# Norms ahead of the weight split in the first block of queries, and the stores of key differences issued by ScalarE

## Chip, cores and metric

The kernel runs on one core of a Trainium2 chip. The metric is the device time of one execution in microseconds (us); lower is better. Before the change three executions took 1596.75, 1595.55 and 1596.62 us, so the median is 1596.62 us.

The core has five engines with a queue of instructions each, which run beside each other and wait for one another by semaphores: TensorE (PE in the profile; PEld is its weight load), VectorE (DVE), ScalarE (ACT), GpSimd (POOL) and SyncE (SP). An engine works through its own queue in order. In this kernel SP does nothing but issue DMA transfers, which move data between the core's memory (SBUF) and the chip's main memory (DRAM).

## What is computed

One transformer layer with adaptive layer norm on 2 x 1024 tokens of width 512: modulated norm, causal attention with 32 query heads and 8 key heads of width 64 and rotary positions, an output projection, a second modulated norm and a feed-forward part with ternary weights.

```python
mod = (_silu(c) @ wmod).reshape(2, 6, 1, -1)          # sa, ca, ga, sb, cb, gb
h = _layernorm(x) * (1 + ca) + sa
q = (h @ Wq) ...; k = (h @ Wk) ...; v = (h @ Wv) ...   # heads of 64
q = apply_rope(q, pos); k = apply_rope(k, pos)
scores = where(causal, q k^T / 8, min)
x = x + ga * (softmax(scores) v) @ Wo
h = _layernorm(x) * (1 + cb) + sb
x = x + gb * rms_norm(silu(h Wg) * (h Wu)) @ Wp        # Wg, Wu, Wp rounded to three levels by groups of 64
```

All of it is in float32. Each float32 operand of a large matrix product is split into a high part (the value rounded to the type float32r, by a copy on ScalarE) and a low part (the value minus its high part, by a subtraction on VectorE or GpSimd); three products of the parts, high x high, high x low and low x high, are summed in PSUM.

## The kernel before

The first stage, some 300 us of the span, makes queries, keys and values and stores them to DRAM for the attention stage, which reads them back in pieces. It works on four blocks of 512 tokens. For each block `keys_values(blk)` makes two tiles of keys (each four heads) and four tiles of values, and then, for blocks 0 to 2, `queries(blk, g)` makes the queries of one group of heads, for g = 0 to 7. The queries of block 3 and everything after are emitted by a planner with costs and due times, which does not see the first stage. The order on each engine in the first stage is the order of the calls in the program.

The steps that matter, by function:

- `load_x(blk)` loads the tokens of a block into the tile xt, one call ahead. `stats(blk, t)` (st, mv) and `rstd(blk)` measure mean and variance on VectorE; ve is the variance plus epsilon, and rs, its power -1/2, is one GpSimd instruction. `norm(blk, t)` normalises 128 tokens in place: one VectorE tensor_scalar on xt with mv and rs. Stats and rstd of the next block run at the end of `keys_values`; the norms of the next block run in the first two groups of queries, two in each (lines 535 to 537).
- `first_T(blk, e)` transposes the normalised xt on TensorE into the PSUM tile pt, in the groups 2 to 5; `first_h` modulates it on VectorE (h), copies the high part on ScalarE (hH) and takes the low part on GpSimd (hL).
- `split_w("wq", n)` splits a 512 KB piece of Wq, which arrives in the buffer stage: high part wqH on ScalarE, low part wqL on VectorE. It runs in block 0 alone, pieces 0 to 3 behind the four value tiles and pieces 4 to 7 in the groups 0 to 3 of queries. Each split frees a buffer, and SP then issues the next load.
- `rope_mm` makes two PSUM tiles pqk of a group or key tile in 24 matrix products; `rope_mul` multiplies them by cosines and sines (four VectorE products ra, rc, rb, rd) and joins them on GpSimd (ra and rc). For keys GpSimd also takes two differences of neighbouring 128-key steps, for the tile of differences kds.
- `rope_end(n)` finishes the group that is one behind: for each of ra and rc a ScalarE copy (rr, high part) and a VectorE subtraction (rr, low part), then four stores by SP (qs or ks). For keys there are more: a second ScalarE copy makes the high part of the differences in place (ra<-rb, rc<-rd), and SP stores it at line 479: two stores for each key tile, four for each block, sixteen in all (eight of 256 KB and eight of 192 KB).
- `value(blk, t)` makes a tile of values in the PSUM tile pv with 12 matrix products; ScalarE copies it to vt (three buffers), and SP stores it (vs).

PSUM tiles come from two rotating sets, four banks for the first half of pqk and small products, three banks for the second half, pt and pv. A bank must be read before TensorE can fill it again: so a copy vt or a product rb, rd that comes late holds TensorE up three tiles later.

The lines that the change touches, before:

```python
479                SY.dma_start(f32(half[:, to:to + 512 - f]), f32(r[:, f:512].bitcast(F32R)))
...
535        if blk < 3 and g < 2:
536            norm(blk + 1, 2 * g)
537            norm(blk + 1, 2 * g + 1)
538        rope_end(1)
```

Of the kernel before, what the change touches and what calls it, by code (L numbers as in the profile page):

```python
# [9 lines left out]
F32R = mybir.dt.float32r  # L10
# [181 lines left out]
def block_kernel(ctx, tc, x, wq, wk, wv, wo, wgu, wpj, cin, wmod, cos, sin, out):  # L192
    nc = tc.nc
    T = InOrder(tc, nc.tensor, True)
    V, A, P, SY = (InOrder(tc, e, False) for e in (nc.vector, nc.scalar, nc.gpsimd, nc.sync))
# [3 lines left out]
    def f32(ap):  # L199
        return ap.bitcast(F32)  # L200
# [51 lines left out]
    def put_q(dst, rr, h, tok):  # L252
        to = f32(dst[h // 2 * 64:h // 2 * 64 + 64, :, h % 2, tok:tok + 512]).rearrange("(c d) l t -> d l c t", c=2)
        SY.dma_start(to, f32(rr[h * 32:h * 32 + 32]).rearrange("d (l c) t -> d l c t", l=2))
# [99 lines left out]
    def mods(i, n):  # L354
        if n == 0:
            mod_row[i] = stile("pm")
        pm = mod_row[i]
        wm = staged.pop(0)
        for k in range(EC):
            T.matmul(pm[k * 32:k * 32 + 32, n * 256:n * 256 + 256], sc[:, k, :], wm[:, k, :], start=True, stop=True)  # L360
        if n == 0:
            stage()
        else:
            mod_row[i] = wm[:, 0:2, :].rearrange("p n e -> p (n e)")
            A.activation(mod_row[i], pm, AF.Copy)

    def mods_T(i):
        pm = stile("pmT")[:, 0:EC * B].rearrange("p (e b) -> p e b", b=B)
        for e in range(EC):
            T.matmul(pm[:, e, :], mod_row[i][:, e * 128:e * 128 + 128], pick, start=True, stop=True)  # L370
        stage()
        if i % 2:
            V.tensor_scalar(modT[:, i], pm, 1.0, None, ALU.add)
        else:
            V.tensor_copy(modT[:, i], pm)
# [9 lines left out]
    def split_w(name, n, width=256):  # L385
        nn = slice(n * width, n * width + width)
        if name == "wq":
            st = staged.pop(0)
        else:
            st = first[name][:, :, nn]  # L390
        split(st, wH[name][:, :, nn], wL[name][:, :, nn])
        if name == "wq":
            stage()
# [17 lines left out]
    def norm(blk, t):  # L411
        d = st_x[blk]
        V.tensor_scalar(d["x"][:, t, :], d["x"][:, t, :], d["mv"][:, t, 0:1], d["rs"][:, t:t + 1], ALU.subtract, ALU.mult)

    def first_T(blk, e):
        d = st_x[blk]
        if e == 0:
            d["h"] = [(hp0, hp1)[blk % 2].tile([128, EC, 512], F32R, name=n) for n in ("hH", "hL")]
        d["pt"] = d.get("pt", {})
        d["pt"][e] = transpose_x(d["x"], 4, e)  # L420

    def first_h(blk, e):
        d = st_x[blk]
        modulate(blk // 2, d["pt"].pop(e), lp, 0, *d["h"], e)
# [3 lines left out]
    def rope_mm(blk, name, c0, dst):  # L428
        hH, hL = st_x[blk]["h"]
        pt = [stile("pqk"), xtile([128, 512], "pqk")] if ropes or blk else [stile("pqk") for half in range(2)]  # L430
        parts = [(w_, h_, k) for w_, h_ in ((wH[name], hH), (wL[name], hH), (wH[name], hL)) for k in range(EC)]
        if not (ropes or blk):
            turns = [(half, part) for k in range(EC) for part in (parts[k], parts[EC + k]) for half in range(2)]
            turns += [(half, part) for part in parts[2 * EC:] for half in range(2)]
        else:
            turns = [(half, part) for half in range(2) for part in parts]
        seen = [0, 0]
        for half, (w_, h_, k) in turns:
            c = c0 + half * 128
            T.matmul(pt[half], w_[:, k, c:c + 128], h_[:, k, :], start=(seen[half] == 0), stop=(seen[half] == 3 * EC - 1))  # L440
            seen[half] += 1
        ropes.append([pt, blk % 2 * 512, dst])

    def rope_mul():
        pt, tok, dst = ropes[-1]
        c_, s_ = cs[:, tok:tok + 512], sn[:, tok:tok + 512]
        a, bb, c, d = (tp.tile([128, 512], F32, name=n) for n in ("ra", "rb", "rc", "rd"))
        V.tensor_tensor(a, pt[0], c_, ALU.mult)
        V.tensor_tensor(c, pt[0], s_, ALU.mult)
        V.tensor_tensor(bb, pt[1], s_, ALU.mult)  # L450
        V.tensor_tensor(d, pt[1], c_, ALU.mult)
        P.tensor_tensor(a, a, bb, ALU.subtract)
        P.tensor_tensor(c, c, d, ALU.add)
        ropes[-1][0] = (a, c)
        if len(dst.shape) == 3:

            ropes[-1][0] = (a, c, bb[:, 0:384], d[:, 0:384])
            for new, r in ((bb, a), (d, c)):
                P.tensor_tensor(new[:, 0:384], r[:, 128:512], r[:, 0:384], ALU.subtract)

    def rope_end(n):
        while len(ropes) > n:
            (a, c, *steps), tok, dst = ropes.pop(0)
            rr = tp.tile([128, 4, 512], F32R, name="rr")
            for i, r in enumerate((a, c)):
                A.activation(rr[:, i, :], r, AF.Copy)
                if not steps:
                    V.tensor_tensor(rr[:, 2 + i, :], r, f32(rr[:, i, :]), ALU.subtract)
                    continue
                V.tensor_tensor(rr[:, 2 + i, 0:128], r[:, 0:128], f32(rr[:, i, 0:128]), ALU.subtract)  # L470
                f, to = (128, 512) if tok else (0, 0)
                if not tok:

                    V.tensor_tensor(r[:, 0:128].bitcast(F32R), r[:, 256:384], f32(rr[:, i, 256:384]), ALU.subtract)
                high = r[:, 128:512].bitcast(F32R)
                A.activation(high, steps[i], AF.Copy)
                V.tensor_tensor(rr[:, 2 + i, 128:512], steps[i], f32(high), ALU.subtract)
                half = [x for pair in kds for x in pair][[x for pair in ks for x in pair].index(dst)][i]
                SY.dma_start(f32(half[:, to:to + 512 - f]), f32(r[:, f:512].bitcast(F32R)))
            for h in (0, 2, 1, 3):  # L480
                if len(dst.shape) == 4:
                    put_q(dst, rr, h, tok)
                else:
                    SY.dma_start(f32(dst[:, h, tok:tok + 512]).rearrange("(c d) t -> d c t", c=4), f32(rr[h * 32:h * 32 + 32]))
# [14 lines left out]
    def keys_values(blk):  # L499
        b = blk // 2  # L500
        if blk < 3:
            load_x(blk + 1)
        for i in range(2):
            rope_mm(blk, "wk", i * 256, ks[b][i])
            if blk == 0:
                split_w("wv", i)
            rope_mul()
            rope_end(1)
        for t in range(4):
            value(blk, t)  # L510
            if blk == 0:
                split_w("wq", t)
            if t == 0:
                rope_end(0)
            if blk < 3:
                stats(blk + 1, t)
        if blk < 3:
            rstd(blk + 1)

    def queries(blk, g):  # L520
        rope_mm(blk, "wq", g * 256, qs[blk // 2][g])
        nxt = blk < 3 and 2 <= g < 6
        if nxt:
            first_T(blk + 1, g - 2)
        if blk == 0 and g < 4:
            split_w("wq", g + 4)
        rope_mul()
        if blk == 1 and g < 2:
            for n in range(2):
                mods(2 + g, n)  # L530
        elif blk == 1 and g in (3, 4):
            mods_T(g - 1)
        if nxt:
            first_h(blk + 1, g - 2)
        if blk < 3 and g < 2:
            norm(blk + 1, 2 * g)
            norm(blk + 1, 2 * g + 1)
        rope_end(1)
# [47 lines left out]
    for blk in range(NT // 512):  # L586
        keys_values(blk)
        if blk < NT // 512 - 1:
            for g in range(KVH):
                queries(blk, g)  # L590
# [13 lines left out]
    tail, outer, norm, rest = ExitStack(), ExitStack(), ExitStack(), ExitStack()  # L604
# [1021 lines left out]
```

## Time and profile before

| | us |
|---|---|
| median of three executions | 1596.62 |
| profiled execution | 1598.2 |
| its span (first to last instruction) | 1596.3 |
| TensorE busy | 1548.1 |
| VectorE busy | 1175.4 |
| GpSimd busy | 863.0 |
| ScalarE busy | 697.8 |

In the timelines below a line has the start in us, the duration in us, the engine (SPq is SP's DMA issues), the line in the program (a helper records every operation, so it is always L39), the operation, what is written from what, its shape, and how many instructions were merged. In square brackets stands the idle time of the engine before it and who ended it. The duration of an issue on SPq is the time that SP's queue was taken by it, not that of the transfer. Durations of neighbours on one engine can overlap a little, as an instruction begins before the last has written its end; the distance of starts is then the better measure.

The table of waits gives, for an engine and what it computed, which instruction ended its idle time: us in total, times, longest. The view by windows gives, for stretches of time, the busy time of each engine, the clock granted to TensorE (1.00 is full speed) and the mean busy share of the 16 DMA engines.

### The profile page before, as it was taken

What the parts mean: (1) busy time and instruction counts of PE and PEld (TensorE: products, weight loads), DVE (VectorE), ACT (ScalarE), POOL (GpSimd) and SP (SyncE); (2) the same over time, 40 slices, a digit from 0 to 9 for tenths busy, and PEclk for the clock granted to TensorE, in tenths of its full rate; (3) what the DMA queues carried; (4) which work ended last, traced back from release to release, by engine and by line L of the source; (5) the groups of instructions that cost most, each with busy time, mean ns of one, the idle gap of its engine ahead of it and who ended that gap; (6) DMA issues with size and microseconds to landing.
All of it is one profiled execution on the core that took longest, in us unless ns stands there. A gap on an engine that the chain in (4) does not pass through costs nothing.

```text
span 1596.3 us, 26757 instructions
## 1 busy us (share of the span) xinstructions
PE 1548.1 (97%) x9028; PEld 1068.0 (67%) x9028; DVE 1175.4 (74%) x2468; ACT 697.8 (44%) x1349; POOL 863.0 (54%) x758
## 2 busy tenths in 40 slices
PE   8899998989999999999999999999999999999998
PEld 7777887745555555555555555477788887888886
DVE  6888887778777788888878888857888674443444
ACT  3322222146555556555555656634655432222221
POOL 4364556537666765765676675713323544444343
PEclk9999999999999999999999999999999999999999
DMA  7775758775555546655646555576777833020000
GB/s 247 243 201 173 225 150 230 227 182 163 154 146 150 143 125 172 167 157 141 169 123 172 146 150 144 161 244 198 251 216 246 288 102 136 1 79 1 11 16 27
DMA packets 206592, 250.55 MB, mean 157 GB/s; under 512 B 34932, under 2 KB 144500, under 8 KB 206456
## 3 DMA queue, kind: packets, MB, share of 16 engines
q1 hardware_dynamic: 206456, 248.85, 53.0%
q8 instruction: 71, 1.16, 0.3%
q14 instruction: 65, 0.53, 0.1%
HBM read 156.24 MB, written 92.02 MB: 156 GB/s over the span
## 4 chain that ended last, share of the span: by engine, by line
PE 70%; DVE 13%; DMA 6%; issue 5%; SPq 3%; ACT 2%; POOL 1%; DVEq 0%; ACTq 0%; POOLq 0%
PE pgu L39 15%; PE po L39 13%; PE pj L39 10%; PE pfo L39 7%; PE pqk L39 6%; PE pm L39 5%; DVE junk L39 3%; SPq L39 3%; PE pr L39 2%; DVE rr L39 2%; DMA k<-ks 1%; DMA t<-qs 1%; DVE mm L39 1%; DVE ra L39 1%; DVE rd L39 1%
## 5 line engine op out<-in xcount | busy, mean ns | idle before, releaser
L39 POOL TENSOR_TENSOR acc<-acc,e 128x512 f32<-128x512 f32 x202 | 266.0, 1328 | 61.6 <-DVE acc L39 47.7
L39 PE MATMUL po<-e,vt 128*64 128x512 f32 (+1 forms) x1280 | 268.0, 557 | 4.2 <-DVE mx L39 1.6
L39 PE MATMUL pgu<-h,gu 128*128 128x512 f32 x1024 | 244.3, 391 | 0.0
L39 PEld LDWEIGHTS pgu<-h,gu 128*128 128x128 f32 x1024 | 192.0, 188 | 39.8
L39 DVE CUSTOM_DVE_ANT_0 junk<-pm,cmask,mm 128x384 bf16<-128x384 f32 (+1 forms) x256 | 174.6, 682 | 57.7 <-PE pm L39 33.2
L39 PEld LDWEIGHTS po<-e,vt 128*64 128x64 f32 x1280 | 84.0, 136 | 154.8 <-issue 123.3
L39 PE MATMUL pm<-k,t 64*128 64x384 f32 (+3 forms) x768 | 167.1, 384 | 16.1 <-DVE mx L39 6.0
L39 POOL TENSOR_SCALAR_AFFINE_SELECT e<-e 128x512 f32<-128x512 f32 x128 | 88.3, 692 | 143.6 <-ACT e L39 140.9
L39 PEld LDWEIGHTS pm<-k,t 64*128 64x128 f32 x768 | 93.5, 185 | 105.6 <-issue 31.6
L39 POOL TENSOR_TENSOR s<-hm 128x512 f32<-128x512 f32 x59 | 68.7, 1164 | 163.3 <-DVE hm L39 163.1
L39 DVE CUSTOM_DVE_ANT_0 junk<-pm,cmask 128x128 bf16<-128x128 f32 (+3 forms) x256 | 124.6, 487 | 41.4 <-PE pm L39 18.8
L39 DVE TENSOR_REDUCE mm<-pm 128x1 f32<-128x384 f32 (+2 forms) x256 | 128.3, 546 | 31.6 <-PE pm L39 31.1
L39 PE MATMUL pj<-woH,oh 128*128 128x512 f32 x512 | 142.2, 399 | 0.0
L39 POOL TENSOR_TENSOR on<-on,ri 128x512 f32<-128x512 f32 x64 | 85.5, 1337 | 66.8 <-DMA ri<-linv 62.7
L39 DVE TENSOR_TENSOR mL<-hm,mH 128x512 fp32r<-128x512 f32 x64 | 75.9, 1186 | 60.7 <-ACT mH L39 60.7
L39 DVE TENSOR_TENSOR hm<-gs,pgu 128x512 f32<-128x512 f32 x64 | 43.9, 686 | 94.3 <-PE pgu L39 89.9
L39 PEld LDWEIGHTS pj<-woH,oh 128*128 128x128 f32 x512 | 95.1, 188 | 20.9 <-issue 2.3
L39 ACT ACTIVATE mH<-hm 128x512 fp32r<-128x512 f32 x64 | 40.4, 632 | 146.1 <-PE pfo L39 133.3
L39 POOL TENSOR_TENSOR ra<-ra,rb 128x512 f32<-128x512 f32 x40 | 51.7, 1291 | 94.4 <-DVE rb L39 82.5
L39 PE MATMUL pfo<-pj,mH 128*128 128x512 f32 x256 | 100.4, 392 | 0.0
L39 PE MATMUL pfo<-pj,mL 128*128 128x512 f32 x256 | 99.7, 389 | 0.0
L39 POOL TENSOR_TENSOR sq<-sq,s 128x512 f32<-128x512 f32 x59 | 80.8, 1369 | 4.5
(1485 smaller groups left out, 3667.6 us busy)
## 6 DMA issues: line engine op xcount, KB each, us to landing
qs<-rr SPq DMA_DIRECT2D x128, 256.0 KB
t<-qs SPq DMA_DIRECT2D x64, 512.0 KB
k<-ks SPq DMA_DIRECT2D x64, 256.0 KB
ri<-linv SPq DMA_DIRECT2D x128, 128.0 KB
os<-on SPq DMA_DIRECT2D x64, 256.0 KB
ks<-rr SPq DMA_DIRECT2D x32, 256.0 KB
w<-in_wgu SPq DMA_DIRECT2D x32, 256.0 KB
gus<-wr SPq DMA_DIRECT2D x32, 256.0 KB
```

Source lines behind the costliest of these rows:

```text
L39: ins = f(*a, **k)
```

## The change

Two edits. In `rope_end` the sixteen stores of the key differences are issued from ScalarE's queue instead of SP's. In `queries`, for block 0 alone, the two norms of the next block's tokens in the groups 0 and 1 stand right behind the call of `rope_mm`, ahead of the split of Wq and of `rope_mul`; in blocks 1 and 2 they stay where they were. No instruction is added or removed, and what is computed is the same.

```diff
@@ rope_end
-                SY.dma_start(f32(half[:, to:to + 512 - f]), f32(r[:, f:512].bitcast(F32R)))
+                A.dma_start(f32(half[:, to:to + 512 - f]), f32(r[:, f:512].bitcast(F32R)))
@@ queries
         nxt = blk < 3 and 2 <= g < 6
+        if blk == 0 and g < 2:
+            norm(blk + 1, 2 * g)
+            norm(blk + 1, 2 * g + 1)
         if nxt:
             first_T(blk + 1, g - 2)
...
-        if blk < 3 and g < 2:
+        if 0 < blk < 3 and g < 2:
             norm(blk + 1, 2 * g)
             norm(blk + 1, 2 * g + 1)
         rope_end(1)
```

On VectorE the order from the end of block 0's values on was: ve, split piece 4, products of group 0, norms 0 and 1, split piece 5, products of group 1, norms 2 and 3, the two subtractions rr of group 0, split piece 6. It becomes: ve, norms 0 and 1, split piece 4, products of group 0, norms 2 and 3, split piece 5, products of group 1, the two subtractions, split piece 6. On ScalarE each store stands directly behind the copy that fills its tile (ra<-rb or rc<-rd), and ahead of rr<-rc or of the copy vt. On SP the sixteen issues are gone, and the others keep their order. TensorE's and GpSimd's orders stay as they were, and so does everything that the planner emits.

## The prediction

> **What bounds the kernel now.** I read the page's shares first: TensorE is busy 97% of the span, so only places where it stands still, and what makes it late there, can move the time. The change touches the projection of keys and queries, which ends near 300 us. So the second view is the table of what TensorE waited for in the first 300 us (total, times, longest, in us).
>
> ```profile
> PE 1548.1 (97%) x9028; PEld 1068.0 (67%) x9028; DVE 1175.4 (74%) x2468; ACT 697.8 (44%) x1349; POOL 863.0 (54%) x758
> ...
> PE pt L39 <- DVE xt L39: 6.0, 3, 4.3
> PE pm L39 <- DMA t<-qs: 5.3, 1, 5.3
> PE pv L39 <- DVE rd L39: 2.0, 1, 2.0
> PE pv L39 <- ACT vt L39: 1.0, 1, 1.0
> ```
>
> Four stops: transposes wait for the last norms at 58.9 to 64.6; the third value tile of block 1 waits for VectorE at 113.90; the last value tile of block 2 waits for ScalarE's copy of the first at 191.08; the attention's first scores wait for loads at 275 to 281. The third view, the order of time on VectorE, says which of them counts.
>
> ```profile
> 52.33 0.17 DVE L39 TENSOR_SCALAR ve<-mv 128x4 f32<-128x4 f32 x1
> 52.41 1.23 DVE L39 TENSOR_TENSOR wqL<-stage,wqH 128x1024 fp32r<-128x1024 f32 x1
> ...
> 55.95 2.63 DVE L39 TENSOR_SCALAR xt<-xt,mv,rs 128x512 f32<-128x512 f32 x2
> ...
> 62.03 2.56 DVE L39 TENSOR_SCALAR xt<-xt,mv,rs 128x512 f32<-128x512 f32 x2
> 64.52 0.68 DVE L39 TENSOR_TENSOR rr<-ra,rr 128x512 fp32r<-128x512 f32 x1
> 65.12 0.68 DVE L39 TENSOR_TENSOR rr<-rc,rr 128x512 fp32r<-128x512 f32 x1
> 65.72 1.21 DVE L39 TENSOR_TENSOR wqL<-stage,wqH 128x1024 fp32r<-128x1024 f32 x1
> ...
> 97.33 1.47 DVE L39 TENSOR_TENSOR rr<-ra,rr 128x512 fp32r<-128x512 f32 x1
> 98.72 1.78 DVE L39 TENSOR_TENSOR rr<-rc,rr 128x512 fp32r<-128x512 f32 x1
> ```
>
> VectorE stands still for nothing but its own partners from 46.37 (the second split of Wq) to 113.85 (rd of the second key tile): its idle there is 1.22 us after each h, for ScalarE's answer to that h, and never for TensorE. TensorE runs ahead, stops at 58.9 and again at 113.90, where VectorE frees a bank. So VectorE sets the end of this stretch. The 4.3 us stop for the norms costs only what it makes VectorE late, which is nothing; TensorE's earlier restart is given back at 113.90.
>
> **A, the four norms move ahead.** The order changes from ve, split, four products, two norms, split, products, two norms, rr pair to ve, two norms, split, products, two norms, split, products, rr pair. Three things follow between 52.41 and the split at 65.72.
> First, the norms need rs, a GpSimd power that before ran behind the split.
>
> ```profile
> 52.58 1.94 POOL L39 TENSOR_TENSOR rs<-ve,mhalf 128x4 f32<-128x4 f32 x1 [14.63 <-DVE ve L39]
> 127.21 1.03 POOL L39 TENSOR_TENSOR rs<-ve,mhalf 128x4 f32<-128x4 f32 x1 [8.95 <-DMA kds<-rc]
> 8.11 0.54 DVE L39 TENSOR_SCALAR xt<-xt,mv,rs 128x512 f32<-128x512 f32 x1
> ```
>
> Now VectorE waits for it, and the split, the products and everything to 113.85 queue behind. By the 1.03 row it ends at 53.61, and VectorE loses 53.65 - 52.41 = 1.24 us (low 1.0 by the 0.78 us rs at 8.27; high 2.16 by its own 1.94). Second, the first two norms leave the joins ra and rc of GpSimd: 2.55 us for the pair beside those joins, about 0.45 each in the opening, where GpSimd is idle (start to start 0.46 from the 8.11 row). That is 2.55 - 0.90 = 1.65 saved. Norms 2 and 3 still follow the products, so they keep 2.55. Third, the joins of group 1 then meet the rr pair instead: 1.20 us at 64.52, 100.42 - 97.33 = 3.09 where that pair runs beside joins. That is 1.89 lost (low 0, if they miss each other). A = 1.24 - 1.65 + 1.89 = +1.5 (from 1.0 - 1.65 = -0.65 to 2.16 - 1.65 + 1.89 = +2.4). The norms end near 60.7, some 4 us earlier for TensorE, and its next stop comes at the bank that the products of group 1 free: no gain at 113.90.
>
> **B, block 0: ScalarE issues four stores of key differences.** Each store waits for the ScalarE copy just before it and then keeps ScalarE's queue for its issue; behind it stand rr<-rc, the copy vt and wqH, for which VectorE waits. No row shows an issue on ScalarE. The nearest are the same stores on SP.
>
> ```profile
> 35.14 0.33 SPq L39 DMA_DIRECT2D kds<-ra  x1
> ...
> 44.07 0.90 SPq L39 DMA_DIRECT2D kds<-ra  x1
> 45.06 0.44 SPq L39 DMA_DIRECT2D kds<-rc  x1
> ...
> 123.08 1.26 SPq L39 DMA_DIRECT2D kds<-ra  x1
> ```
>
> 0.33 where SP had been idle; 0.40 to 1.26 (mean of the twelve 0.80) while other issues crowd. I take 0.33 for the uncrowded and 0.56, the middle of 0.33 and 0.80, for the crowded, since part of the 0.80 may belong to SP's own queue; and 0.10 more each, because ScalarE's copies overlap by that (42.10 + 0.53 against 42.53). First tile: the issue behind ra (+0.43) is mostly covered by VectorE's rr<-rb at 35.14 (0.92 us) and leaves 0.2; the issue behind rc costs 0.43 in full: 0.65 late at wqH. Second tile: 2 x 0.66 = 1.3. B = +2.0 at the split of 46.37, from which VectorE is bound (0.4 if only the overlap is lost; 0.65 + 2 x 1.36 = 3.4 at most).
>
> **C, block 1.** Again two crowded issues stand before the copy vt of the second value tile (123.04, done 123.57), and TensorE needs that bank at 121.09 + 2.72 = 123.81 for the second half of group 0. Slack 0.24: 2 x 0.66 - 0.24 = +1.1 (0 to 2.5 by 1.26 each). VectorE then waits for TensorE at 133.44, so it passes on.
> **D, block 2.** TensorE's 1.01 us wait at 191.08 is for vt, behind one more uncrowded issue: +0.4 (0 to 1.0). The second tile's issues fall into a slack of about 1.4 us.
> **E, block 3 and the loads.** SP is rid of two kds issues (264.31 to 265.93, so 1.6 us) before the loads of the attention, which are issued from 271.58. But the sixteen DMA engines show a share of 0.91 to 1.15 in every 2 us from 262 to 280: the loads wait for bytes, and these are the same. Only 260 to 262 (0.32) has room: -0.5 (from -1.6, the whole lead, to 0). Without this cover of bytes the lead would be worth its 1.6.
>
> Sum: 1.5 + 2.0 + 1.1 + 0.4 - 0.5 = +4.5. On the profiled execution: span 1596.3 to 1600.8, with the 1.9 around it 1598.2 to 1602.7. The median, 1596.62, lies 1.6 below that run: 1601.1.
>
> **The skill against the trace.** "Perfetto Trace Analysis", section "DMA Instruction — HWDGE (DVE, Sync)", says that two issuing queues share one descriptor generator, and one waits while the other has it; the trace has a single issuing queue and can't show it. By that page the crowded issues would cost about SP's 0.80, and the four of B and C, 0.24 more each, would make the sum 1.0 higher. For the clock, the row first: after the 2.00 us stop at 113.90 the granted clock reads 0.57 and 0.58 until 119, and 24 products take 7.19 us (113.90 to 121.09) where the next 24 take 5.44; after the 1.01 us stop it stays 1.00. "TensorE: Matmul & The Clock Gate", section "Part 1: The HAM clock gate", puts the drop at an idle window of about 3.4 us; then a stop grown from 2.0 to 5.5 would newly cost 1.75. By the row that is already paid, and I add nothing.
>
> **Rivals.**
> *ScalarE's issues are nearly free* (only 0.1 of overlap each): A 1.5 + B 0.4 + 0 + 0 - 0.5 = +1.4, 1598.0. For it: the 0.33 rows, and ScalarE's 44% share. Against: its queue is in order, and VectorE waits on exactly these copies. 0.15.
> *Issues collide with SP's* at 1.26: 1.5 + 3.4 + 2.5 + 1.0 = +8.4, 1605.0. For it: SP stores ks and vs in those very microseconds. Against: 0.40 rows lie among them. 0.14.
> *Not slower: SP's shorter queue brings the attention's loads forward.* Place: the 5.3 us stop before 280.5. Price: up to -1.6 there. It decides once A to D come to less than 1.6; at their low ends (-0.65 + 0.4) the sum is -1.85, 1594.8, and if the stop at 113.90 then shrinks towards the 1.01 that kept its clock, another 1.75 goes: 1593.0. For it: those loads are issued after 12 us of unbroken SP issues. Against: the DMA shares above. 0.19.
>
> **How the numbers follow.** Forecast 0.52, around 1601.1, its own range 1599.0 to 1603.5. A measurement of this kernel tells about 0.2%, 3.2 us, from no change: slower is above 1599.8, faster below 1593.4. Slower: 0.48 of the forecast and 0.14. Same: 0.04 of the forecast, 0.15, and 0.04 of the last rival; the other 0.15 is faster. Range 1592.5 to 1606.0: it takes in the rivals' ends and leaves out about 0.1 beyond.
>
> **What would show it.** A: VectorE idle about 1.2 us for POOL rs, norm pair 0.9, rr pair near 3.1, TensorE's stop for norms about 2 us. B: the split of 46.37 about 2 us later. C: a new TensorE wait for vt near 124 plus the lag. The stop at 113.90 longer by A + B, 5.5 us. E: loads issued about 2 us sooner after the last keys, landing hardly sooner. It is wrong if ScalarE's issues show under 0.2 us, if rr runs beside joins at 0.68, or if the stop before the first scores shrinks by over 1.5 us.

## The result and the profile after

The changed kernel takes 1602.4 us (median of 19 executions, 1600.53 to 1609.73) against 1597.75 for the kernel before (19 executions, 1594.45 to 1603.57). The ratio is 1.0031, with a 95% interval of 1.0021 to 1.0041: about 5 us (4.65 at the medians) slower. Its profiled execution spans 1599.1 us, 2.8 more than that of before.

The opening, up to the last split of Wv (wvL), is of different length from one execution to the next: that split starts at 28.00 us in the profile of before, at 27.41 in a second profile of the same kernel, and at 26.65 and 27.25 in two of the changed kernel. So below I count from the start of that split ("from wvL"). The first scores (pm<-k,t) stand in the first profile of before and in that of the changed kernel at

```profile
280.49 0.44 PE L39 MATMUL pm<-k,t 64*128 64x128 f32 x1 [5.27 <-DMA t<-qs]
```

```profile
283.59 0.44 PE L39 MATMUL pm<-k,t 64*128 64x128 f32 x1 [5.29 <-DMA t<-qs]
```

From wvL that is 252.49 us before and 256.94 after; the second profiles have 252.85 and 257.98. In the mean the scores come 4.8 us later, about as much as the medians differ. (The two spans differ by less, 2.8, because the opening of this execution was 1.35 us shorter.)

From the page of the changed kernel, busy us, share and instructions of each engine:

```profile
PE 1550.4 (97%) x9028; PEld 1071.0 (67%) x9028; DVE 1173.5 (73%) x2468; ACT 699.1 (44%) x1349; POOL 862.8 (54%) x758
```

The work is that of before within a few us. What changed is where TensorE stands still; its table of waits in the first 300 us (total, times, longest):

```profile
PE pm L39 <- DMA t<-qs: 5.3, 1, 5.3
PE pt L39 <- DVE rd L39: 3.3, 2, 2.7
PE pt L39 <- DVE xt L39: 2.4, 3, 1.2
PE pv L39 <- DVE rd L39: 2.3, 2, 2.0
PE pv L39 <- ACT vt L39: 2.0, 2, 1.5
```

The wait of the transposes for the norms (xt) fell from 6.0 to 2.4 us, but the bank that rd frees came in its place (3.3). The wait for vt doubled (1.54 at 193.87, and 0.50 at 38.43, where the second profile of before has 1.33 too, so only the first is a mark of the change). The stop for the loads before the first scores stayed at 5.3. VectorE's timeline at the moved norms:

```profile
53.85 1.00 DVE L39 TENSOR_SCALAR xt<-xt,mv,rs 128x512 f32<-128x512 f32 x2 [1.14 <-POOL rs L39]
54.77 1.22 DVE L39 TENSOR_TENSOR wqL<-stage,wqH 128x1024 fp32r<-128x1024 f32 x1
...
58.30 2.57 DVE L39 TENSOR_SCALAR xt<-xt,mv,rs 128x512 f32<-128x512 f32 x2
...
64.33 1.44 DVE L39 TENSOR_TENSOR rr<-ra,rr 128x512 fp32r<-128x512 f32 x1
65.69 1.77 DVE L39 TENSOR_TENSOR rr<-rc,rr 128x512 fp32r<-128x512 f32 x1
67.38 1.21 DVE L39 TENSOR_TENSOR wqL<-stage,wqH 128x1024 fp32r<-128x1024 f32 x1
```

The three terms of A can be read off: 1.14 us idle for rs; a first pair of norms of 0.92 (53.85 to 54.77), while the second, beside GpSimd's joins, keeps 2.50; and an rr pair of 3.05 (64.33 to 67.38) that took 1.20 before. ScalarE's timeline at the second key tile of block 0 (ACTq is its queue of issues):

```profile
41.28 0.53 ACT L39 ACTIVATE ra<-rb 128x384 fp32r<-128x384 f32 x1 [1.43 <-DVE ra L39]
41.83 0.33 ACTq L39 DMA_DIRECT2D kds<-ra  x1
42.21 0.63 ACT L39 ACTIVATE rr<-rc 128x512 fp32r<-128x512 f32 x1 [0.41 <-ACT ra L39]
44.08 0.52 ACT L39 ACTIVATE rc<-rd 128x384 fp32r<-128x384 f32 x1 [1.23 <-DVE rc L39]
44.63 0.33 ACTq L39 DMA_DIRECT2D kds<-rc  x1
45.00 0.60 ACT L39 ACTIVATE vt<-pv 128x512 f32<-128x512 f32 x1 [0.40 <-ACT rc L39]
```

The first and the third of these rows, before:

```profile
42.10 0.53 ACT L39 ACTIVATE ra<-rb 128x384 fp32r<-128x384 f32 x1 [1.43 <-DVE ra L39]
42.53 0.62 ACT L39 ACTIVATE rr<-rc 128x512 fp32r<-128x512 f32 x1
```

From the start of one copy to that of the next it is 42.21 - 41.28 = 0.93 us; before it was 42.53 - 42.10 = 0.43. One issue in ScalarE's queue costs the copy behind it 0.50 us. The issue itself shows 0.33 or 0.34 in all sixteen rows. Eight of them overlap an issue of SP's, as the one at 41.83 does, where SP is in the middle of an issue of 0.94 (41.71).

### The profile page after: what moved, and what is told of

The parts are those of the page before. It is cut to its first block, busy times and chain, and to the rows that moved or that the text cites. A ratio compares the mean times of both kernels' runs of the same rounds, so it can differ in the third digit from the quotient of the medians.

```text
span 1599.1 us, 26751 instructions
## 1 busy us (share of the span) xinstructions
PE 1550.4 (97%) x9028; PEld 1071.0 (67%) x9028; DVE 1173.5 (73%) x2468; ACT 699.1 (44%) x1349; POOL 862.8 (54%) x758
## 4 chain that ended last, share of the span: by engine, by line
PE 70%; DVE 13%; DMA 6%; issue 6%; ACT 3%; SPq 1%; POOL 1%; ACTq 0%; DVEq 0%; POOLq 0%
PE pgu L39 15%; PE po L39 14%; PE pj L39 10%; PE pfo L39 7%; PE pm L39 5%; PE pqk L39 4%; DVE junk L39 3%; PE pr L39 3%; DVE rr L39 2%; SPq L39 1%; DMA k<-ks 1%; DVE mm L39 1%; DVE rd L39 1%; DMA qs<-rr 1%; DVE ra L39 1%
## 5 line engine op out<-in xcount | busy, mean ns | idle before, releaser
L39 POOL TENSOR_TENSOR ra<-ra,rb 128x512 f32<-128x512 f32 x40 | 51.7, 1293 | 97.1 <-DVE rb L39 89.4
```

The lines of the kernel that those rows point to most:

```text
L39: ins = f(*a, **k)
```

## The experiments

Each run is timed against the kernel before on the same chip (its medians: 1598.45 in 29 executions for the first four runs, 1596.58 in 24 for the next four, 1597.47 and 1597.60 in 17 for the later two). Executions of one kernel spread over 3 to 14 us, so where two runs differ by less than 2 us I read the stages and not the times.

### Each half of the change alone

First the norms ahead, with the stores left on SP; the diff is against the changed kernel.

```diff
-                A.dma_start(f32(half[:, to:to + 512 - f]), ...)
+                SY.dma_start(f32(half[:, to:to + 512 - f]), ...)
```

> The four norms ahead, all stores issued by SP. Theory (VectorE sets the end of this stretch; the norms cost it 1.2 us of waiting for rs, save 1.6 us beside idle GpSimd, and lose 1.9 us where the joins then meet the rr pair): +1.5 us against before, split piece 6 and the product rd of block 1's second key tile 1.4 to 1.7 us later after the split of piece 1 than before, TensorE's stop for the norms down to about 2.4 us in all, its stop for rd at the third value tile of block 1 moved by the same 1.5. Rival 1 (an earlier restart of TensorE is a gain): 2 to 4 us faster than before. Rival 2 (all of the loss is ScalarE's issues): within 0.5 us of before.

Measured: 1597.51 us, ratio 0.9994 (0.9981 to 1.0007). VectorE reaches split 6 (the split of Wq's piece 6) 1.46 us later than before, as A said, and the program is not slower. TensorE's timeline of this run, the stops at the third value tile of block 1, the last one of block 2, and the first scores:

```profile
114.09 1.21 PE L39 MATMUL pv<-wvH,hH 128*128 128x512 f32 x4 [1.98 <-DVE rd L39]
...
189.78 1.21 PE L39 MATMUL pv<-wvH,hH 128*128 128x512 f32 x4 [1.01 <-ACT vt L39]
...
278.01 0.44 PE L39 MATMUL pm<-k,t 64*128 64x128 f32 x1 [4.05 <-DMA t<-qs]
```

From wvL (26.78) these are 87.31, 163.00 and 251.23. Before they were 85.90, 163.08 and 252.49. So 1.4 us late at the first, nothing at the second: the lag is gone between them, and the theory that VectorE's lag runs on to the end misses.

Then the issues alone, with the norms where they were; the diff is against the kernel before.

```diff
-                SY.dma_start(f32(half[:, to:to + 512 - f]), ...)
+                A.dma_start(f32(half[:, to:to + 512 - f]), ...)
```

> The sixteen stores issued by ScalarE, norms as before. Theory (each issue holds ScalarE's queue 0.33 us and breaks an overlap of 0.10, and in each block some of these stand on the path): 1.5 in block 0, 0.6 in block 1, 0.5 in block 2, 0.3 in block 3: +2.9 us against before. Rival 1 (a second queue of transfers delays the loads and stores of the first): +2.9 too, but seen as later landings, not as later copies on ScalarE. Rival 2 (all of the loss is the norms): within 0.5 us of before.

Measured: 1603.75 us, ratio 1.0030 (1.0015 to 1.0045); first scores 255.58 from wvL, 2.9 later than the mean of the two profiles of before. The split of piece 0 is 0.53 late and that of piece 1 1.54, one issue and three, as B's mechanism wants. By the times the issues carry the loss and the norms add nothing that can be told.

### Where the issues cost: late, doubled, and by block

The same sixteen issues on ScalarE, but later in its queue, where the data has long been ready: in block 0 behind the splits 1, 2 and 3, in the others behind the copies vt.

```diff
-                SY.dma_start(f32(half[:, to:to + 512 - f]), ...)
+                late.append(lambda ...: A.dma_start(...))
...
+            for _ in range((0, 1, 1, 2)[t] if blk == 0 else (2, 0, 2, 0)[t]):
+                late.pop(0)()
             if t == 0:
                 rope_end(0)
```

> The sixteen stores issued by ScalarE, but later in its queue: in block 0 behind the second, third and fourth split (one, one, two), in the other blocks behind the copies of the first and the third value tile (two each); norms as before. Theory (only the place in ScalarE's queue costs): 0 to +0.6 us against before, and up to 0.5 faster if SP's shorter queue helps the loads. Rival (the second queue of transfers costs): +2.9 us as with the stores in their first place.

Measured: 1603.01 us, ratio 1.0023 (1.0008 to 1.0037), against an expectation of almost nothing. The splits of pieces 2 and 3, which stand behind late issues, start 20.33 and 22.27 us from wvL as before, and that of piece 4 0.14 late: in that place the issues cost ScalarE's copies next to nothing. The first loss comes from SP. Its waits in the first 300 us hold a new line, and the timeline shows the effect, a load that comes late:

```profile
SPq L39 <- DMA kds<-rc: 6.0, 2, 5.0
```

```profile
46.44 7.18 SPq L39 DMA_DIRECT2D ks<-rr  x4
...
54.53 1.21 SPq L39 DMA_DIRECT2D stage<-in_wq  x1
...
60.34 1.06 ACT L39 ACTIVATE wqH<-stage 128x1024 fp32r<-128x1024 f32 x1 [6.90 <-DMA stage<-in_wq]
```

One of SP's four stores of keys waits 5.0 us for the landing of a store of ScalarE's. The compiled program says why: the transfers of both queues share eight DMA semaphores in the order of the program, and each transfer waits for the one that used its semaphore before. One of these four stores carries a wait on the semaphore of a kds<-rc, which ScalarE issues late. So the load of Wq's piece 5 goes out 25.6 us from wvL (54.53 - 28.92) instead of 22.7, and split 5 is 2.0 us late. Taking the issues out of ScalarE's way put them into SP's. That is not the whole loss of this run: its first scores come at 257.10, 4.4 us late. Another 1.5 is lost in block 1, where TensorE's clock drops on the path (in the part on the clock below); the rest isn't taken apart.

The same coupling is in the changed kernel, where SP's table of waits holds

```profile
SPq L39 <- DMA kds<-rc: 2.9, 4, 1.0
SPq L39 <- DMA kds<-ra: 1.6, 3, 0.8
```

and nothing of the kind before. In block 0 the load of piece 5 then goes out 0.6 us later (23.28 from wvL instead of 22.69), and VectorE doesn't wait for that piece at split 5, so there it is off the path.

Next each store as two of 64 partitions, so twice the issues for the same bytes.

```diff
-                A.dma_start(f32(half[:, to:to + 512 - f]), f32(r[:, f:512].bitcast(F32R)))
+                A.dma_start(f32(half[0:64, to:to + 512 - f]), f32(r[0:64, f:512].bitcast(F32R)))
+                A.dma_start(f32(half[64:128, to:to + 512 - f]), f32(r[64:128, f:512].bitcast(F32R)))
```

> The sixteen stores issued by ScalarE as thirty-two, each with half of the partitions, so the bytes and the queue are the same; norms as before. Theory (0.35 to 0.4 us of ScalarE's queue for each issue on the path): about +3 more than with sixteen, +6 us against before. Rival (second queue of transfers): +2.9 us as with sixteen.

Measured: 1612.33 us, ratio 1.0094 (1.0069 to 1.0120): +14, more than twice the +6 expected. In ScalarE's timeline two issues take more than twice the 0.33 of one:

```profile
43.24 1.39 ACTq L39 DMA_DIRECT2D kds<-ra  x2
44.68 0.63 ACT L39 ACTIVATE rr<-rc 128x512 fp32r<-128x512 f32 x1 [1.47 <-issue]
```

The copy stands 1.47 us, where a single issue cost it 0.41. The direction is the theory's; the size isn't, so this run doesn't measure the single issue. Part of the excess may be SP's: it waits 14.5 us for landings of ScalarE's stores here, against 4.5 in the changed kernel, and the run doesn't tell the two apart.

Then the issues by block: block 0 on ScalarE and the rest on SP, and the reverse.

```diff
-                SY.dma_start(f32(half[:, to:to + 512 - f]), ...)
+                (A if not tok and any(dst is k for k in ks[0]) else SY).dma_start(f32(half[:, to:to + 512 - f]), ...)
```

> Edit against the kernel before: ScalarE issues the four stores of key differences of block 0 alone, in the place that the change gives them; the other twelve stay on SP. Theory (each issue in its place holds ScalarE's queue 0.33 + 0.1 us, and VectorE behind it where it is the bound, and each block pays once): the split of piece 1 comes 1.5 us later, block 2's last value tile and the first scores 1.5 later as well, time +1.5 (ratio 1.0005 to 1.0015). Rival (block 0's lag is caught up at the stop before the first scores, and the cost comes from the copies vt of blocks 1 and 2): split 1 1.5 later, but time within 0.5 us of before. Second rival (the cost comes with each transfer on a second queue, wherever it is): a quarter of the whole, +1.2.

> Edit against the kernel before: ScalarE issues the twelve stores of key differences of blocks 1, 2 and 3, and SP keeps the four of block 0. Theory: split 1 where it was; a new wait for vt near 124 us (0.3 to 1.4), 1.5 us longer at block 2's last value tile, and time +1.5 to +3 (ratio 1.001 to 1.002). Rival (block 0 pays, the others have slack): time within 0.5 us of before. Second rival (each transfer on a second queue costs alike, and SP waits for ScalarE's landings through the shared semaphores): three quarters of the whole, +3.6, with waits of SP for the stores kds in the list.

Measured: block 0 alone 1602.04 us, ratio 1.0028 (1.0015 to 1.0040); blocks 1 to 3 alone 1603.57, ratio 1.0036 (1.0023 to 1.0049). Against before that is +5.5 and +7.0, more than twice the whole, with 6 and 5 executions. The stages are finer, us from wvL:

| run | TensorE restarts, third value tile of block 1 | first copy rr of the second key tile, block 1 | last value tile of block 2 | first scores |
|---|---|---|---|---|
| before | 85.90 | 92.76 | 163.08 | 252.49 |
| before again | 85.92 | 93.29 | 163.62 | 252.85 |
| norms alone | 87.31 | 92.68 | 163.00 | 251.23 |
| issues, block 0 | 87.43 | 93.57 | 163.90 | 253.17 |
| issues, blocks 1 to 3 | 85.87 | 93.33 | 165.19 | 255.21 |
| issues, all | 87.41 | 94.25 | 166.15 | 255.58 |
| changed kernel | 88.85 | 95.36 | 167.22 | 256.94 |
| changed again | 88.88 | 95.94 | 167.78 | 257.98 |

From the second column to the third it takes 70.32 or 70.33 in the four runs whose issues of blocks 1 to 3 stand on SP, and 71.84 to 71.90 in the four whose issues stand on ScalarE: 1.5 us, which is three issues at 0.50. That is C and D, two issues ahead of vt in block 1 and one in block 2, and it comes whatever else is changed.

The parts can be seen singly: where TensorE waits for vt at the second half of pqk in block 1, it restarts 2.90 us behind the copy rr with those issues on SP and 3.93 or 3.94 with them on ScalarE, and its wait for vt at block 2's last value tile is 1.01 or 1.02 in the first four and 1.53 or 1.54 in the others. The second rival of the run with blocks 1 to 3, SP's waits for ScalarE's landings, has its sign in the list as well (4.1 us); but between the copy rr and vt there is only ScalarE's own queue, so the 1.5 isn't theirs. Whether they add to the 2.5 by which that run's first scores are late is open.

Block 0's issues and the norms each make VectorE 1.4 to 1.5 us late in the first column, and of either alone no more than 0.5 is left in the second. Of both together (2.95) there are 2.3 and 2.9 left.

The times don't follow the stages one to one: +5.5 against a stage of +0.5 in the block-0 run, +7.0 against +2.5 with blocks 1 to 3, +5.3 against +2.9 with all issues. The stages come from one profile of each run, and outside the stage executions differ as well (wvL starts between 26.65 and 31.86 us in the profiles of this document). Where the issues cost is shown by the stages; why these times are longer than that is open.

### Is the clock a part of it?

The kernel before and the changed one once more, unchanged, for second profiles.

> The kernel before once more, for a second profile: how much of a profiled difference is a matter of the execution? Theory: from the last split of Wv to the first scores it takes 252.5 us where the clock drops behind the stop of 2.0 us at the third value tile of block 1 (a loss of 1.7), and about 250.8 where it doesn't; the waits there (2.0, vt 1.0, t<-qs near 5) are those of the first profile within 0.2. Rival (stage times differ by 2 us and more from one execution to the next whatever the clock does): a stage time outside 250.3 to 253.0, or other waits.

> The changed kernel once more. Theory (a drop of the clock behind the stop at 115.5 and the wait for the copies vt hide each other): if the clock drops again, 256.9 us from the last split of Wv to the first scores, with one wait for vt of about 0.35 in block 1; if it doesn't, waits for vt of 1.7 to 2.6 in block 1 in place of the drop, and again 256 to 257.5. Rival (the drop is a loss of its own): without it the stage takes 255.2, with 0.35 for vt.

TensorE's timeline of the kernel before, second time:

```profile
113.33 1.19 PE L39 MATMUL pv<-wvH,hH 128*128 128x512 f32 x4 [1.85 <-DVE rd L39]
...
116.63 1.20 PE L39 MATMUL pv<-wvH,hH 128*128 128x512 f32 x4 [0.28 <-ACT vt L39]
...
123.60 1.20 PE L39 MATMUL pqk<-hH,wqH 128*128 128x512 f32 x4 [1.22 <-ACT vt L39]
```

Here four products take 1.07 to 1.20 behind the stop, where they took up to 1.91 in the first profile: the clock didn't drop. But TensorE then waits 0.28 + 1.22 = 1.50 us for vt, which it hadn't before, and the first scores come at 252.85 instead of the 250.8 that my theory expected. So in the kernel before the drop cost next to nothing: it filled time in which TensorE would have waited for vt. In the changed kernel the clock dropped both times; its wait for vt at the second half of pqk was 0.35 and 0.90. In its second profile the scores come at 257.98, 1.1 later than expected with a drop. So I have not seen the changed kernel without a drop, and that part of the theory wasn't tried.

A drop isn't free everywhere. In the run with the late issues it came behind the wait for vt at the second half of pqk, so nothing was left to fill:

```profile
127.54 1.19 PE L39 MATMUL pqk<-hH,wqH 128*128 128x512 f32 x4 [1.81 <-ACT vt L39]
128.57 1.54 PE L39 MATMUL pqk<-hH,wqL 128*128 128x512 f32 x4
129.91 1.91 PE L39 MATMUL pqk<-hL,wqH 128*128 128x512 f32 x4
```

The granted clock is 0.63 and 0.52 in the 4 us from 128.5. From that restart to the next group's products it takes 5.51 us there (127.54 to 133.05) and 3.97 in the second profile of before, and all of the 1.5 is still there at block 2's last value tile.

### What sets vt, and a version that is faster

The first copy rr of the second key tile, which the vt of block 1 stands behind, waits in these profiles for "DMA qs<-rr": the stores of group 7's queries, which must land before its buffer rr is free. They stand on SP behind the loads of the next tokens. Four versions, all with the stores of key differences on SP, were meant to be faster. The first puts the four norms behind split 4:

```diff
-        if blk == 0 and g < 4:
+        if blk == 0 and g < 4 and g != 1:
             split_w("wq", g + 4)
+        if blk == 0 and g == 0:
+            for t in range(4):
+                norm(1, t)
         rope_mul()
+        if blk == 0 and g == 1:
+            split_w("wq", g + 4)
...
-        if blk < 3 and g < 2:
+        if 0 < blk < 3 and g < 2:
```

> Edit against the kernel before: all four norms in group 0, behind split 4 and ahead of the products of group 0; split 5 moves behind the products of group 1; stores stay on SP. Theory (VectorE sets the end of the stretch to 113.9 us, and the three terms of A are what a place for the norms is worth): here rs is ready before the norms start, so the wait of 1.14 us goes, and four norms instead of two run beside idle GpSimd (2 x 0.9 instead of 0.9 + 2.6): the split of piece 6 comes 1.5 to 2.5 us sooner than in the kernel before, and the program takes 1594 to 1597 (0.9975 to 0.9995). Rival (what VectorE gains or loses before 113.9 is given back by the stop before the first scores, as with the norms alone): the split of piece 6 moves as in the theory, but the time stays within 1 us of before (ratio 0.9995 to 1.0005) and the stop for t<-qs is 1.5 to 2.5 us longer than 5.3. Second rival (the four norms hold back the first products and so the banks that TensorE needs): TensorE stops for rd or rb 2 us longer in group 0, ratio 1.001.

Measured: 1597.27 us, ratio 1.0004 (0.9994 to 1.0014), a miss. The four norms took 1.83 us (56.69 to 58.52), but VectorE still stood 0.92 for rs, and the split and the first subtraction rr, which now met GpSimd's joins, took 2.10 and 1.77. Split 6 gained 0.24.

The second puts the statistics into VectorE's gaps in block 0 and the norms among the splits:

```diff
                 A.activation(high, steps[i], AF.Copy)
+                if fill and not tok:
+                    fill.pop(0)()
...
+            if blk == 0 and t == 0:
+                rstd(1)
+            if blk == 0 and t:
+                norm(1, t - 1)
...
```

> Edit against the kernel before: the statistics of the next tokens go into the four VectorE gaps of about 0.65 to 1.2 us that the keys of block 0 leave while ScalarE copies the differences; rstd stands behind the first value tile, and the four norms among the splits of Wq, where GpSimd does nothing; stores stay on SP. Theory (VectorE sets the end of this stretch): VectorE reaches split 6 some 3.5 to 4.5 us sooner, TensorE's stop for the norms goes, and the program takes 1593 to 1596 (ratio 0.996 to 0.9985). Rival (the loads before the first scores set the end of the stage): the lead is there at split 6, but the stop for t<-qs grows from 5.3 by all of it, ratio 0.9995 to 1.0005. Second rival (the tokens of block 1 land too late for statistics so early): VectorE waits for xt by DMA, the splits come later than in the kernel before, ratio above 1.001.

Measured: 1597.56 us, ratio 1.0002 (0.9990 to 1.0015), a miss too; its first scores come 1.5 us sooner (251.17), which the time doesn't show. Its timeline shows the load of piece 5 issued on SP, its split by ScalarE, and VectorE behind it:

```profile
50.41 0.94 SPq L39 DMA_DIRECT2D stage<-in_wq  x1
...
56.98 1.06 ACT L39 ACTIVATE wqH<-stage 128x1024 fp32r<-128x1024 f32 x1 [6.82 <-DMA stage<-in_wq]
...
58.08 1.23 DVE L39 TENSOR_TENSOR wqL<-stage,wqH 128x1024 fp32r<-128x1024 f32 x1 [3.32 <-ACT wqH L39]
```

VectorE stood ready for 3.32 us, and a transfer that had been hidden became the bound. The third version adds the remedy: in block 0 SP issues the six stores of the second key tile behind the loads of Wq. Its `store` puts what `rope_end` stores in a list and issues it only while nothing is held; the list is emptied behind the last value tile of the block.

```diff
             if t == 0:
+                hold[0] = blk == 0
                 rope_end(0)
+                hold[0] = False
...
+            while held:
+                SY.dma_start(*held.pop(0))
...
```

> Edit against the kernel before: the statistics and norms as in the run with the statistics in the gaps, and in block 0 SP issues the six stores of the second key tile behind the loads of Wq's pieces 5 to 7 instead of ahead of them. Theory (with the statistics in the gaps VectorE stood still 3.32 us at split 5 for piece 5, whose load stood on SP behind those stores and was issued 3.3 us after its buffer came free): piece 5 lands near 54 us instead of 57, VectorE's wait at split 5 goes, split 6 comes 3 to 3.7 us sooner than in the kernel before (counted from the last split of Wv), the first scores 3 to 4.5 us sooner, and the program takes 1592 to 1594.5 (ratio 0.997 to 0.9988). Rival (the load is slow because the DMA engines are full, not because it is issued late): it is issued 3 us sooner and lands less than 1 us sooner, split 5 as before, ratio 0.9995 to 1.0005. Second rival (the lead is given back at the stop for t<-qs): split 6 some 3 us sooner, but that stop grows by as much, ratio 0.9995 to 1.0005.

Measured: 1595.63 us, ratio 0.9991 (0.9978 to 1.0004). In its timeline the load goes out at 47.09 and has landed by 52.45:

```profile
47.09 0.38 SPq L39 DMA_DIRECT2D stage<-in_wq  x1
...
52.45 1.06 ACT L39 ACTIVATE wqH<-stage 128x1024 fp32r<-128x1024 f32 x1 [2.49 <-DMA stage<-in_wq]
...
57.47 0.69 DVE L39 TENSOR_TENSOR ra<-pqk,cs 128x512 f32<-128x512 f32 x1 [0.87 <-DMA kds<-ra]
```

Split 6 is 2.2 us sooner than before (0.87 went to the held store, which must land before ra is written again), the first scores 3.3 (249.38 from wvL). The last version also moves the token loads of blocks 1 and 2 behind group 7's stores:

```diff
-        if blk < 3:
+        if blk == 0:
             load_x(blk + 1)
...
             rope_end(1)
+            if i == 0 and 0 < blk < 3:
+                load_x(blk + 1)
```

> Edit against the run with early loads: in blocks 1 and 2 SP issues the four loads of the next tokens behind the stores of group 7's queries instead of ahead of them. Theory (TensorE's wait for the copy vt in block 1 hangs on ScalarE's first copy of the second key tile, and that on the landing of group 7's stores, which free its buffer and stand on SP behind 3.7 us of token loads): that copy, at 89.97 us from the last split of Wv, starts 2 to 3.5 us sooner, the wait for vt of 0.75 at the second half of pqk goes, the 1.04 at block 2's last value tile shrinks, the first scores come 1 to 2.5 us sooner, and the program takes 1591.5 to 1595 (ratio 0.996 to 0.9985). Rival (the copy waits for VectorE and GpSimd, and the stores' landing is only the last of several by a little): the copy starts less than 1 us sooner, vt as before, time as in the run with early loads. Second rival (the tokens come late for their statistics): VectorE waits for xt, and the ratio is 0.9995 or above.

Measured: 1595.56 us, ratio 0.9986 (0.9971 to 1.0000). ScalarE's copy, in the run with early loads and then in this one:

```profile
117.42 0.63 ACT L39 ACTIVATE rr<-ra 128x512 fp32r<-128x512 f32 x1 [3.76 <-DMA qs<-rr]
```

```profile
114.34 0.63 ACT L39 ACTIVATE rr<-ra 128x512 fp32r<-128x512 f32 x1 [1.70 <-POOL rd L39]
```

From wvL that is 89.97 and 87.61, so 2.4 us sooner, and now GpSimd's rd ends the wait: the copy did hang on the landing of those stores. The wait for vt in block 1 is gone, and the first scores come at 247.16. The wait of 1.03 in block 2 stayed, against the expectation. In the first two of the four versions the clock dropped behind the stop in block 1 with no wait for vt to fill, in the last two it didn't; by the 2.90 from copy to restart I estimate the drop's part at 1.4 and 0.9 us in the first two. The stage of this last one gains 5.5 us on before and the time 2.0 at the medians; the interval still touches 1.0, so this version points to a gain and doesn't prove one.

## Why the prediction came out, point by point

The forecast, 1601.1 us and slower, held: 1602.4. It was +4.5 on the median of three executions of before, and +4.65 was measured on that of 19; the stage grew by 4.8 us. The terms were not all right, though: A and B together came out 0.9 smaller than their sum, and E 1.1 larger, with the other sign. That these two errors cancelled is luck.

**A, norms ahead, +1.5.** Right on VectorE: 1.14 idle for rs, a pair of 0.92, an rr pair of 3.05, split 6 1.46 late when alone. What failed is the step "VectorE sets the end of this stretch", by which a lag there runs on in full. With the norms alone nothing of it was left at the copy of the second key tile, because that copy waits for a transfer ("DMA qs<-rr", 3.07 us in that run). Only on top of B's lag does it show.

**B, block 0's issues, +2.0.** The mechanism is right, the size was off: the crowded price of 0.66 (0.56 for the issue and 0.10 of lost overlap) measured 0.50, the same as the uncrowded one, which I had at 0.43. Three issues at 0.50 are 1.5, and 1.54 was measured at split 1: the first tile's issue behind ra, for which I left 0.2, is hidden (the copy rc<-rd behind it starts 10.21 us from wvL, 10.19 before, as it waits for VectorE both times). The Trainium skill has it that one of two issuing queues waits while the other has the descriptor generator ("Perfetto Trace Analysis", section "DMA Instruction — HWDGE (DVE, Sync)"). By that the prediction estimated 0.80 for them; the sixteen rows of 0.33 and 0.34, eight of them beside an issue of SP's, show no such wait in ScalarE's queue.

**A and B together** (+3.5 by their terms) measured 2.95 at the bank that VectorE frees and 2.6 (mean of 2.3 and 2.9) at the copy.

**C, block 1, +1.1; D, block 2, +0.4.** Measured 1.0 and 0.5 (2.90 to 3.93, and 1.01 to 1.53). But C's reason was incomplete: not a slack of 0.24 at 123.81 in one execution, but the chain from group 7's stores to the copy to vt carries it. So the visible wait for vt was only 0.35, and yet the full price was paid.

Together that is 2.6 + 1.0 + 0.5 + 0.6 for what follows = 4.7 of the 4.8.

**E, loads sooner, -0.5.** This step failed, in its sign: "SP is rid of two kds issues ... before the loads of the attention". It is, but SP's own issues took longer. SP's timeline of the changed kernel:

```profile
268.19 4.16 SPq L39 DMA_DIRECT2D ks<-rr  x4
272.44 2.49 SPq L39 DMA_DIRECT2D vs<-vt  x3
275.02 0.71 SPq L39 DMA_DIRECT2D k<-ks  x1
```

The four stores take 4.16 us where they took 3.09, and from the first of them to the load it is 6.83 instead of 5.65. Most of the 1.43 that the two issues of that tile took is given back. From block 2's last value tile to the first scores, the runs with the later blocks' issues on ScalarE took 89.4 to 90.2 (mean 89.8), the two profiles of before 89.4 and 89.2: +0.5 (+0.6 in the two of the changed kernel), of which 0.29 is a new wait for rd in block 3. The size is loose, since the norms alone took 88.2 and block 0's issues alone 89.3; but none of the runs with the later issues on ScalarE took less than any of the others in the table. So the third rival had no ground: the shorter queue on SP brought nothing forward.

**The stop at 113.90.** "Longer by A + B, 5.5 us" was wrong: it stayed 2.00 (115.50). TensorE had been held up earlier, by the waits for rd of 2.71 and 0.61 at 71.04 and 85.61, and arrived as late as VectorE. "By the row that is already paid", said of the clock, came out for the sum, but not for the reason given: the drop filled time in which TensorE would have waited for vt.

**The rivals.** That ScalarE's issues are nearly free fell with the 0.50 in every block; that they collide with SP's at 1.26 fell with the 0.33 of their rows.

## What to carry to other kernels

In this kernel an issue in the queue of an engine that computes cost the next instruction its full time, and more (0.50 for an issue of 0.33), wherever that queue was on the path; so look for what stands behind the issue, not for the engine's busy share. Before adding up lags, look at the next join of the path: a chain bound by a transfer swallows a lag of an engine up to its slack, and two lags that vanish alone can add up when together. And when an engine is made faster, the next bound may be a load that stood unnoticed in a queue behind stores.

## What the runs showed of the hardware

A stop of TensorE of about 2.0 us is no sure sign of a clock drop. Behind the stop at the third value tile of block 1 it dropped in the first profile of before (2.00), in both of the changed kernel (2.00 and 1.97) and in two other runs (1.97 and 1.98), and did not in six runs with stops of 1.98 to 2.00. The length of the stop doesn't decide; what does wasn't found. The Trainium skill puts the drop behind an idle window of about 3.4 us ("TensorE: Matmul & The Clock Gate", section "Part 1: The HAM clock gate"). All of these stops are shorter, and five of them were followed by a drop, so here the measurement decides: a stop need not last that long.

VectorE's norms took 0.46 us each with GpSimd idle and 1.25 beside its joins (0.92 and 2.50 a pair). The eight DMA semaphores that two queues share in this program let a late issue on one engine hold up another engine's queue for 5.0 us.
